# Another written-out order for the 425 pieces of layer 0, on one core

## The chip, the cores and the metric

One core of one Trainium2 chip runs the whole program in one launch. The metric is device microseconds of that core, lower is better. The engines are TensorE (PE, with its weight loads as PEld), VectorE (DVE), ScalarE (ACT), GpSimd (POOL) and SyncE (SP), which in this kernel issues nearly all DMAs. Each engine runs its own instructions strictly in the order in which the program wrote them; engines wait for each other by semaphores.

## The reference, cut to what matters

Two transformer layers with modulated layer norms, for 4 batches of 512 tokens of 512 features, in float32. The change touches the first layer alone:

```python
mod = (silu(L0_c) @ L0_wmod)            # six rows of 512 per batch: sa ca ga sb cb gb; the same for layer 1
h = layernorm(x) * (1 + ca) + sa
q, k, v = h @ Wq + bq, h @ Wk + bk, h @ Wv + bv   # 32 query heads of 16, one key and value head of 16
p = softmax(sum over heads of q (16) times k (16) per token * 1/4)   # a 16 x 16 softmax in each token
x = x + ga * repeat(p @ v, 32)
h = layernorm(x) * (1 + cb) + sb
hits = softmax(h @ centroids.T / 0.1) > 0.01      # 64 clusters
out = where(any hit of the token and any hit of the row's cluster, h @ weight.T + bias, 0)
x = x + gb * out
```

Layer 1 (grouped attention with 32 heads of 128 on 256-wide halves of the weights, then a gated feed-forward) follows, and takes over nine tenths of the time.

## The kernel before

Layer 0 is cut into 425 pieces, each a method of a class `Pieces` (L393 to L780). A string holds them in one order, and the program emits them in just that order under a manual schedule; nothing reorders them afterwards:

```python
def play(order):
    for o in order:
        name, _, eng = o.partition("/")
        name, *numbers = name.split(".")
        getattr(first_pieces, name)(*map(int, numbers), *([eng] if eng else []))
```

So the string is five queues folded into one: for each engine, the pieces that run on it, in the order in which they stand. What a piece waits for is found when it is emitted (data written by another piece, or a buffer still read by one). A piece that must wait holds up everything behind it on its engine, and nothing on the others that does not need it.

In a name such as `xn.1.2.3` the numbers are: the norm (1 before attention, 2 before the feed-forward, 3 the first norm of layer 1), the batch, and the tile or chunk of 128. In `M.0.4` they are the layer and which of the six modulation rows. The batches go in the order 0, 2, 1, 3. A suffix `/d` puts a piece on DVE.

| engine | pieces, with the line that the profile shows |
|---|---|
| SP, issue of DMAs | `x` a batch of the input, 1 MiB (L401; `x.0` is issued by ACT) · `wm.l.j` a modulation weight, 1 MiB (L406, three buffers, so each waits for the `M` that read the one three before) · `c` the two condition inputs (L396, L397) · `wq`, `wkv`, `wffn`, `cent`, `b2`, `asg` weights and small inputs · `gw` writes a gate row to DRAM (L546), `gs` reads it back spread over all partitions (L154) · `wl` first raw weights of layer 1 |
| PE | `M` modulation product (L494) · `MT` its transpose (L509) · `T` four 128 x 128 transposes of the normed x (L596) · `Q` narrow q, k, v product (L373, with h1n) · `Qt` back to tokens (L388) · `oT` (L684) · `ad` attention output spread into two tiles (L695) · `L`, `Lt` the same as `Q`, `Qt` for the clusters · `G` gate row (L538) · `F` feed-forward product of a tile, nine matmuls (L751, L755) · `hit`, `rs` |
| DVE | `st` layer-norm statistics of a tile (L62, L63) · `ve`, `nm` (L570, L579) · `silu` (L455 to L457) · `wcat`, `bcat`, `biasr` weight and bias preparation (L461, L466, L472 to L475) · `mo`, `gr` modulation and gate rows (L522, L530 to L533) · `qe`, `s`, `mx`, `den`, `rec`, `os`, `o` the small softmax (L632, L640, L649, L662, L671, L675, L678) · `xa` adds into x (L701) · `lm`, `ld`, `qs`, `fs`, `sel`, `cs` |
| ACT | `siluexp` (L451) · `xn` normed tile (L587) · `ev` a transposed chunk out of PSUM, modulated (L618; `/d` L616) · `pc`, `qc`, `lc`, `oe`, `gc`, `re` copies out of PSUM (L360) · `exp`, `le` |
| POOL | `pw` power -0.5 of the variance (L574) · `sub`, `mul` of the small softmax (L653, L666) · `R` masks a gate row (L557) · `asgf` · `fa` adds x (L765; `/d` on DVE) |
| ACT, POOL and SP | `ws` one step of the split of layer 1's weights |

Buffers that bind: PSUM has two banks for `Q`, `Qt`, `MT`, `G`, `L`, `Lt`, three for `M` (a pair of rows each), `ad` and `F`, two for `T` and `oT`. The normed tiles of norm 1 have one buffer, so `xn.1` of a batch waits for the last `T.1` of the batch before. In `modT` the rows `mo.0.0` and `mo.0.1` are what every `ev.1` needs. `R.b` needs the gate row that `gs.0.2.b` brings, and `ad.b` needs both `R.b` and `oe.b`.

After the string a short second list (four more `T`, `F`, `fs` and `fa`) leads over into layer 1, whose work is written by other code (from L1327) that the change does not touch.

## Time and profile before

| | |
|---|---|
| time, median of 3 runs | 1996.34 us (1993.04 to 2001.08) |
| the profiled execution | 1994.15 us, its span 1992.1 us |
| mean granted TensorE clock | 0.994 |
| PE busy over the span | 1943.3 us, 98% |
| DVE, ACT, POOL busy | 1185.3, 1105.1, 969.2 us |
| first PE instruction | 13.35 us |
| first matmul of layer 1 (L919) | 175.13 us |

The span is the time from the first to the last instruction of the profiled execution; some 2 us lie around it. Times inside the profile are microseconds from the start of the span. Layer 0 is the stretch up to about 175 us. A row of the timeline merges neighbouring instructions of one line: start, length, engine and line, operation, output and input, count, and in brackets the idle time before it with what ended that.

### The profile page before, as it was taken

The page shows a single profiled execution, that of the slowest core. Times are in us where ns is not written, and L with a number is a line of the kernel's source. Part 1 is how long each engine was busy: PE and PEld are TensorE (multiplying, and loading weights), DVE is VectorE, ACT ScalarE, POOL GpSimd, SP SyncE. Part 2 cuts the span into 40 slices and gives each one's busy share as a digit, 9 for nine tenths or more (in the row PEclk, how much of TensorE's full clock was granted, in tenths as well). Part 3 has the DMA queues.
Part 4 walks back from the last instruction along what each step waited for, and adds up shares of the span by engine and source line. Part 5 has one row for each costly group of instructions (what it writes and reads, how often), then busy time and mean ns, then how long its engine had stood idle before and what let it go on. Part 6 is the DMA issues. An engine that isn't in the chain of part 4 may idle for free.

```text
span 1992.1 us, 27490 instructions
## 1 busy us (share of the span) xinstructions
PE 1943.3 (98%) x8543; PEld 1466.5 (74%) x8543; DVE 1185.3 (60%) x3128; ACT 1105.1 (55%) x2541; POOL 969.2 (49%) x778
## 2 busy tenths in 40 slices
PE   5899899999999999999999999999999999999998
PEld 2345677777777777777777777777777778788887
DVE  5767655655656675565566655656555564655544
ACT  4434866666665666666666656665666652332322
POOL 2315555555557655555675555558555543711010
PEclk9799999999999999999999999999999999999999
DMA  9302667676567766656677665666656566501000
GB/s 317 113 27 74 182 166 185 161 188 167 149 161 184 188 180 170 163 153 163 179 193 197 158 164 149 151 156 179 166 142 164 136 157 216 169 26 33 25 25 23
DMA packets 268652, 293.84 MB, mean 148 GB/s; under 512 B 27218, under 2 KB 224914, under 8 KB 268500
## 3 DMA queue, kind: packets, MB, share of 16 engines
q1 hardware_dynamic: 267972, 290.97, 54.9%
q8 instruction: 71, 1.16, 0.2%
q10 hardware_dynamic: 528, 1.05, 0.1%
q14 instruction: 81, 0.66, 0.1%
HBM read 142.99 MB, written 11.57 MB: 78 GB/s over the span
## 4 chain that ended last, share of the span: by engine, by line
PE 89%; POOL 3%; DMA 3%; SPq 2%; DVE 2%; issue 1%; ACT 0%; ACTq 0%; DVEq 0%; POOLq 0%
PE quarter L862 19%; PE av L1067 14%; PE x L919 14%; PE sc L1018 13%; PE p L902 8%; PE p_up L1586 4%; PE p_gate L1586 4%; PE acc L1605 4%; PE x L902 3%; PE ffn L751 3%; SPq L1057 2%; PE narrow L373 1%; DMA x<-in_L_attn_x_dram 1%; PE lnT L596 1%; PE add_ps L695 1%
## 5 line engine op out<-in xcount | busy, mean ns | idle before, releaser
L1021 DVE CUSTOM_DVE_ANT_0 sc<-sc,mask 128x512 f32<-128x512 f32 (+3 forms) x512 | 250.0, 488 | 261.4 <-PE sc L1018 261.3
L1018 PE MATMUL sc<-kT,qT 128*128 128x512 f32 (+3 forms) x1024 | 359.2, 433 | 0.0
L1067 PE MATMUL av<-x,v 128*128 128x512 f32 x1008 | 292.2, 433 | 1.7 <-DMA x<-x 1.2
L1067 PEld LDWEIGHTS av<-x,v 128*128 128x128 f32 x1008 | 188.3, 189 | 111.1 <-issue 61.2
L1035 ACT ACTIVATE p<-p,sums 128x512 f32<-128x512 f32 (+3 forms) x256 | 143.1, 559 | 120.9 <-DVE sums L1034 120.7
L1018 PEld LDWEIGHTS sc<-kT,qT 128*128 128x128 f32 x1024 | 186.5, 190 | 30.0 <-issue 0.7
L988 DVE TENSOR_TENSOR acc<-acc,quarter 128x512 f32<-128x512 f32 x196 | 134.5, 686 | 105.9 <-PE quarter L862 105.8
L310 POOL TENSOR_TENSOR lo_qa<-raw,hi_qa 128x512 fp32r<-128x512 f32 x64 | 81.6, 1276 | 236.4 <-ACT hi_qa L309 182.1
L1035 ACT ACTIVATE x<-x,sums 128x512 f32<-128x512 f32 (+3 forms) x256 | 142.8, 558 | 83.2 <-DVE sums L1034 83.2
L862 PEld LDWEIGHTS quarter<-wo,oT 128*128 128x128 f32 x720 | 136.4, 190 | 49.1 <-issue 24.4
L862 PE MATMUL quarter<-wo,oT 128*128 128x256 f32 x720 | 170.2, 379 | 0.3 <-ACT oT L1072 0.3
L1024 ACT ACTIVATE x<-sc,sums 128x512 f32<-128x512 f32 (+3 forms) x256 | 133.4, 521 | 42.0 <-DVE sums L1021 39.3
L1038 DVE STREAM_TRANSPOSE p<-p 128x512 f32<-128x512 f32 (+3 forms) x256 | 129.1, 504 | 45.8 <-ACT p L1035 45.7
L1038 DVE STREAM_TRANSPOSE x<-x 128x512 f32<-128x512 f32 x248 | 125.6, 506 | 36.9 <-ACT x L1035 36.0
L1024 ACT ACTIVATE p<-sc,sums 128x512 f32<-128x512 f32 (+3 forms) x256 | 132.0, 516 | 14.7 <-DVE sums L1021 14.6
L310 POOL TENSOR_TENSOR lo_qb<-raw,hi_qb 128x512 fp32r<-128x512 f32 x64 | 82.0, 1283 | 115.5 <-ACT hi_qb L309 112.0
L931 DVE SCALAR_TENSOR_TENSOR qT<-p,qT 128x512 f32<-128x512 f32 x128 | 88.0, 690 | 81.1 <-PE p L902 81.1
L1072 ACT COPY oT<-av 128x512 f32<-128x512 f32 x128 | 74.5, 582 | 84.8 <-PE av L1067 84.6
L320 POOL TENSOR_TENSOR hi_qa<-hi_qa,lo_qa 128x512 fp32r<-128x512 f32 x64 | 82.5, 1290 | 75.6 <-PE x L919 75.3
L320 POOL TENSOR_TENSOR hi_qb<-hi_qb,lo_qb 128x512 fp32r<-128x512 f32 x64 | 82.9, 1296 | 66.6 <-PE x L919 64.2
L862 PE MATMUL quarter<-so,soT 128*128 128x256 f32 x480 | 113.5, 379 | 0.0
L298 ACT ACTIVATE lo_kv<-lo_kv 128x512 fp32r<-128x512 f32 x64 | 40.2, 628 | 128.4 <-POOL lo_kv L310 128.4
(265 smaller groups left out, 4295.3 us busy)
## 6 DMA issues: line engine op xcount, KB each, us to landing
x<-p SPq DMA_DIRECT2D x512, 128.0 KB, 2.6
x<-x SPq DMA_DIRECT2D x496, 128.0 KB, 2.8
raw<-in_L_attn_w_q_dram SPq DMA_DIRECT2D x128, 256.0 KB, 3.2
wo<-in_L_attn_w_o_dram SPq DMA_DIRECT2D x30, 1024.0 KB, 5.9
wm<-in_L_wmod_dram SPq DMA_DIRECT2D x12, 1024.0 KB, 9.7
raw<-in_L_attn_w_k_dram SPq DMA_DIRECT2D x32, 256.0 KB, 3.8
raw<-in_L_attn_w_v_dram SPq DMA_DIRECT2D x32, 256.0 KB, 4.0
xn<-x_d SPq DMA_DIRECT2D x28, 256.0 KB, 4.7
```

The lines of the kernel that those rows point to most:

```text
L310: nc.gpsimd.tensor_tensor(lo, w, hi.bitcast(F32), SUB)
L320: nc.gpsimd.tensor_tensor(hi, hi.bitcast(F32), lo.bitcast(F32), SUB)
L862: nc.tensor.matmul(ps[:, m, :], l[:, k, m * P : (m + 1) * P], r[:, k, :], start=(k == 0), stop=(k == 1),)
L902: nc.tensor.matmul(ps[:, m * width : (m + 1) * width], still(l, k, m), moving(r, k), start=(i == 0 and k == 0), stop=(i == len(pairs) - 1 ...
L919: nc.tensor.matmul(banks[j], l[:, k, cols], r[:, k, :], start=(half == k == 0), stop=(half == 1 and k == KC - 1),)
L1018: nc.tensor.matmul(ps[:, :w], q[:, i * P : w], kT[n][:, :w], start=True, stop=True)
L1021: nc.vector.tensor_tensor_reduce(ps[:, :w], ps[:, :w], mask[:, S - w :], -1.0, -NEG, ADD, ALU.min, nmx)
L1024: nc.scalar.activation(blocks(s, i), ps[:, :w].rearrange("p (j q) -> p j q", q=BK), AF.Exp, bias=nmx, scale=-1.0, accum_out=den,)
L1035: nc.scalar.mul(p, p, rden)
L1038: nc.vector.transpose(blocks(s, i), blocks(s, i))
L1067: nc.tensor.matmul(av.rearrange("p (a n) -> p a n", a=NG)[:, :, BK * k :], vs[n][:, k, :], pT[:, k, :, P * (s % 2) + BK * k : P * (s % 2 + ...
L1586: nc.tensor.matmul(ps[kind], w[kind][:, k, c * P : (c + 1) * P], h2[b % 2][i][:, k, :], start=(k == 0 and i == 0), stop=(k == KC - 1 and i ...
```

## The change

The string of the order is replaced. It holds the same 425 pieces with the same suffixes, each once, so that every instruction and every transfer is issued as before, by the same engine; only their order on the five queues differs, and with it which buffer each one finds free. Nothing else in the program is changed.

```diff
@@ -781,39 +781,37 @@
 
 
     order = """
-    wm.0.0 x.0 st.1.0.1 c st.1.0.3 st.1.0.2 siluexp st.1.0.0 wm.0.1 ve.1.0 pw.1.0 x.2 silu nm.1.0
-    x.1 M.0.0 st.1.2.0 xn.1.0.0 M.0.1 st.1.2.1 xn.1.0.2 st.1.2.2 wkv wm.0.2
-    st.1.2.3 xn.1.0.1 ve.1.2 pc.0.1 wq MT.0.1 mo.0.1 mo.0.0 xn.1.0.3 pw.1.2 T.1.0.0 T.1.0.1 ev.1.0.0 b2
-    bcat ev.1.0.1 wm.0.3 wm.0.4 M.0.2 st.1.1.3 T.1.0.2 st.1.1.0 ev.1.0.2 x.3 T.1.0.3
-    wcat nm.1.2 ev.1.0.3/d st.1.1.2 M.0.3 xn.1.2.0 xn.1.2.2 xn.1.2.3 xn.1.2.1 st.1.1.1 ve.1.1 pw.1.1
-    Q.0 wm.1.0 pc.0.3 T.1.2.0 T.1.2.1 qc.0 MT.0.3 mo.0.3 gr.0.2 Qt.0 qe.0 wm.1.3 ev.1.2.0 G.0.2 gc.0.2 M.0.4
-    s.0 ev.1.2.1 T.1.2.2 st.1.3.1 gw.0.2 st.1.3.0 T.1.2.3 ev.1.2.3 cent nm.1.1 mx.0 gs.0.2.0 ev.1.2.2 st.1.3.3
-    Q.2 M.1.0 wm.1.4 sub.0 st.1.3.2 xn.1.1.0 xn.1.1.1 qc.2 pc.1.0 exp.0 xn.1.1.3 xn.1.1.2 Qt.2 MT.1.0 mo.0.4 mo.1.0 qe.2
-    biasr R.0 den.0 mul.0 wm.0.5 T.1.1.0 ev.1.1.0 T.1.1.1 s.2 ve.1.3 asg gs.0.2.2 ev.1.1.1 M.1.3
-    T.1.1.2 os.0 rec.0 o.0 oT.0 oe.0 mx.2 ev.1.1.2/d pw.1.3 sub.2 T.1.1.3 ad.0.0 exp.2 M.1.4 xa.0.0 xa.0.1
-    ev.1.1.3 nm.1.3 den.2 ad.0.1 xn.1.3.0 xn.1.3.2 gs.0.2.1 Q.1 xn.1.3.1 mul.2 st.2.0.0 rec.2
-    xa.0.3 xn.1.3.3 xa.0.2 qc.1 asgf pc.1.4 R.2 T.1.3.0 ev.1.3.0 wm.1.5 Qt.1 os.2
-    st.2.0.3 o.2 st.2.0.2 st.2.0.1 qe.1 oT.2 s.1 mx.1 wm.1.2 M.0.5 wffn MT.1.4 mo.1.4 mo.1.3
-    T.1.3.1 sub.1 gs.0.2.3 oe.2 wm.1.1 ve.2.0 T.1.3.2 ev.1.3.1 M.1.5 ev.1.3.2
-    pc.1.5 exp.1 den.1 rec.1 MT.1.5 gr.0.5 G.0.5 gc.0.5 gw.0.5 pw.2.0 mul.1 T.1.3.3 ad.2.0 gr.1.5 nm.2.0
-    ev.1.3.3 xn.2.0.0 Q.3 xa.2.0 xa.2.1 xn.2.0.2 G.1.5 qc.3 xn.2.0.3 st.2.2.0 xn.2.0.1 gc.1.5 gw.1.5
-    os.1 R.1 ad.2.1 Qt.3 st.2.2.1 o.1 T.2.0.0 xa.2.2 ev.2.0.0 xa.2.3 oT.1 T.2.0.1 oe.1
-    ad.1.0 T.2.0.2 st.2.2.2 qe.3 st.2.2.3 ev.2.0.1 xa.1.1 s.3 ve.2.2 ev.2.0.2 xa.1.0 T.2.0.3
-    ad.1.1 pw.2.2 xa.1.3 nm.2.2 ev.2.0.3 gs.0.5.0 mx.3 xa.1.2 M.1.2 xn.2.2.0 M.1.1 xn.2.2.2 L.0
-    st.2.1.2 xn.2.2.3 xn.2.2.1 R.3 F.0.3 lc.0 sub.3 gs.0.5.2 st.2.1.0 T.2.2.0 st.2.1.1
-    Lt.0 pc.1.1 lm.0 exp.3 st.2.1.3 T.2.2.1 le.0 den.3 ld.0 ev.2.2.0 ev.2.2.1 ve.2.1 F.0.1
-    T.2.2.2 MT.1.1 rec.3 mul.3 os.3 pw.2.1 T.2.2.3 o.3 F.0.0 ev.2.2.2 nm.2.1 hit.0 ev.2.2.3 qs.0
-    mo.1.1 gr.1.2 oT.3 xn.2.1.0 fs.0.3 xn.2.1.3 L.2 oe.3 fs.0.1 fs.0.0 xn.2.1.1 xn.2.1.2 ad.3.0 lc.2 gs.0.5.3
-    xa.3.0 T.2.1.0 G.1.2 gc.1.2 ad.3.1 Lt.2 xa.3.3 T.2.1.1 xa.3.1 F.0.2 lm.2 xa.3.2 le.2 st.2.3.3
-    st.2.3.2 ev.2.1.1 T.2.1.2 st.2.3.1 st.2.3.0 F.2.2 ev.2.1.2 ve.2.3 pw.2.3 gw.1.2 ld.2 fa.0.1/d
-    T.2.1.3 nm.2.3 ev.2.1.0 xn.2.3.0 F.2.0 qs.2 xn.2.3.3 xn.2.3.2 xn.2.3.1 ev.2.1.3/d T.2.3.0
-    L.1 fs.0.2 T.2.3.1 fa.0.0 F.2.1 lc.1 ev.2.3.0 T.2.3.2 fs.2.2 hit.2 ev.2.3.1 fa.0.2/d
-    fa.0.3/d ev.2.3.2/d T.2.3.3 Lt.1 ev.2.3.3 L.3 fa.2.2 lm.1 F.2.3 lc.3 le.1
-    gs.0.5.1 onehot Lt.3 ld.1 wl fs.2.0 hit.1 lm.3 le.3 F.3.0 ld.3 hit.3
-    fs.2.1 fs.2.3 F.3.2 qs.3 fs.3.0 qs.1 cs fa.3.0/d fa.2.0/d rs fa.2.3/d re sel.0.2 fs.3.2
-    F.1.1 sel.0.3 F.1.0 st.3.0.3 fa.2.1 sel.0.0 sel.0.1 F.1.2 ws st.3.0.1 st.3.0.2 st.3.0.0 sel.2.1
-    sel.2.3 ve.3.0 pw.3.0 ws sel.2.0 fs.1.1 ws fa.3.2/d nm.3.0 fs.1.2 F.1.3 xn.3.0.0 fa.1.2/d
-    fs.1.0 xn.3.0.1 xn.3.0.3 xn.3.0.2 ws T.3.0.0 T.3.0.2 sel.2.2
+    x.0 wm.0.0 x.2 st.1.0.2 st.1.0.1 c siluexp silu st.1.0.3 b2 st.1.0.0 M.0.0 ve.1.0 pw.1.0 st.1.2.1
+    nm.1.0 st.1.2.2 wm.0.1 xn.1.0.0 st.1.2.0 biasr xn.1.0.2 x.1 M.0.1 st.1.2.3 pc.0.1 xn.1.0.3 ve.1.2
+    MT.0.1 st.1.1.3 xn.1.0.1 T.1.0.0 wq pw.1.2 T.1.0.2 mo.0.0 mo.0.1 ev.1.0.0 wcat wm.0.2 T.1.0.3
+    ev.1.0.3/d nm.1.2 st.1.1.2 ev.1.0.2 st.1.1.1 st.1.1.0 ve.1.1 T.1.0.1 M.0.2 wkv ev.1.0.1 xn.1.2.2 Q.0
+    xn.1.2.3 bcat xn.1.2.1 wm.0.3 qc.0 wm.0.4 x.3 M.0.3 pw.1.1 xn.1.2.0 Qt.0 nm.1.1 qe.0 T.1.2.2 pc.0.3
+    ev.1.2.2 T.1.2.3 s.0 mx.0 wm.1.0 MT.0.3 T.1.2.1 ev.1.2.3 T.1.2.0 ev.1.2.1 gr.0.2 ev.1.2.0 M.0.4
+    G.0.2 wm.1.3 xn.1.1.0 mo.0.3 gc.0.2 sub.0 st.1.3.1 Q.2 exp.0 qc.2 st.1.3.0 wm.1.4 st.1.3.2 M.1.0
+    Qt.2 den.0 rec.0 pc.1.0 xn.1.1.1 qe.2 gw.0.2 s.2 xn.1.1.3 MT.1.0 mul.0 mx.2 M.1.3 gs.0.2.0 xn.1.1.2
+    os.0 T.1.1.1 T.1.1.3 o.0 ev.1.1.1 T.1.1.2 gs.0.2.2 ev.1.1.3 ev.1.1.2/d st.1.3.3 oT.0 oe.0 sub.2
+    exp.2 mo.1.0 wm.0.5 R.0 M.1.4 ve.1.3 den.2 T.1.1.0 ev.1.1.0 ad.0.0 pw.1.3 Q.1 wm.1.2 rec.2 pc.1.4
+    xa.0.1 ad.0.1 xa.0.0 nm.1.3 mo.0.4 xn.1.3.1 wm.1.5 qc.1 M.0.5 Qt.1 mul.2 st.2.0.0 st.2.0.1 xn.1.3.3
+    M.1.5 os.2 o.2 xn.1.3.0 xn.1.3.2 xa.0.3 qe.1 oT.2 s.1 R.2 oe.2 T.1.3.1 mx.1 pc.1.5 xa.0.2 T.1.3.0
+    ev.1.3.0 ev.1.3.1 st.2.0.2 wffn st.2.0.3 sub.1 MT.1.5 wm.1.1 T.1.3.2 ve.2.0 ev.1.3.2 ad.2.0 asg
+    xa.2.1 T.1.3.3 gs.0.2.3 pw.2.0 ev.1.3.3 M.1.2 exp.1 M.1.1 xa.2.0 nm.2.0 pc.1.1 MT.1.4 gs.0.2.1
+    xn.2.0.3 ad.2.1 xn.2.0.0 mo.1.3 mo.1.4 st.2.2.1 Q.3 xn.2.0.1 R.1 xn.2.0.2 qc.3 den.1 gr.0.5 xa.2.3
+    T.2.0.2 xa.2.2 mul.1 gr.1.5 os.1 T.2.0.3 ev.2.0.2 cent st.2.2.2 G.0.5 rec.1 o.1 ev.2.0.3 T.2.0.1
+    st.2.2.0 ev.2.0.1 T.2.0.0 ev.2.0.0 Qt.3 qe.3 F.0.3 gc.0.5 st.2.2.3 ve.2.2 oT.1 s.3 pw.2.2 oe.1
+    MT.1.1 G.1.5 ad.1.1 nm.2.2 gc.1.5 mx.3 xa.1.2 xa.1.3 L.0 ad.1.0 xn.2.2.1 sub.3 xn.2.2.2 xn.2.2.0
+    st.2.1.2 xn.2.2.3 xa.1.1 xa.1.0 exp.3 den.3 st.2.1.0 T.2.2.1 st.2.1.3 T.2.2.0 mo.1.1 gw.0.5 F.0.1
+    ev.2.2.0 mul.3 T.2.2.3 ev.2.2.1 T.2.2.2 st.2.1.1 ve.2.1 lc.0 os.3 ev.2.2.3 ev.2.2.2 pw.2.1 gs.0.5.0
+    gs.0.5.2 Lt.0 rec.3 lm.0 gw.1.5 nm.2.1 le.0 xn.2.1.3 xn.2.1.2 F.0.0 o.3 R.3 ld.0 oT.3 L.2 asgf qs.0
+    xn.2.1.1 fs.0.3 xn.2.1.0 oe.3 T.2.1.0 fs.0.1 ad.3.1 xa.3.2 ev.2.1.0 T.2.1.2 T.2.1.1 xa.3.3 ev.2.1.2
+    fs.0.0 st.2.3.3 ad.3.0 lc.2 onehot xa.3.1 st.2.3.2 fa.0.1/d F.0.2 T.2.1.3 ev.2.1.1 st.2.3.1 xa.3.0
+    ev.2.1.3/d st.2.3.0 fs.0.2 Lt.2 ve.2.3 gr.1.2 pw.2.3 nm.2.3 xn.2.3.2 xn.2.3.1 F.2.0 lm.2 F.2.2
+    xn.2.3.3 xn.2.3.0 G.1.2 le.2 gc.1.2 L.1 T.2.3.0 ld.2 lc.1 T.2.3.3 hit.2 ev.2.3.0 Lt.1 gs.0.5.3 lm.1
+    T.2.3.2 ev.2.3.3 T.2.3.1 ev.2.3.1 ev.2.3.2/d gs.0.5.1 F.2.1 qs.2 fs.2.2 L.3 le.1 gw.1.2 fa.0.2/d
+    F.2.3 fs.2.0 lc.3 ld.1 fa.0.0 Lt.3 hit.0 fa.2.0/d lm.3 wl le.3 F.3.0 fs.2.1 ld.3 hit.3 qs.3 fa.2.1
+    fs.3.0 hit.1 fs.2.3 cs ws ws fa.2.3/d fa.0.3/d F.3.2 rs F.1.2 fa.2.2 fs.3.2 re qs.1 F.1.0 sel.0.3
+    sel.0.2 sel.0.1 st.3.0.3 st.3.0.1 st.3.0.2 sel.0.0 st.3.0.0 sel.2.2 ve.3.0 fs.1.2 fa.3.0/d F.1.1
+    pw.3.0 nm.3.0 F.1.3 sel.2.1 fa.1.2/d xn.3.0.2 ws fa.3.2/d xn.3.0.1 fs.1.0 sel.2.3 xn.3.0.3 xn.3.0.0
+    fs.1.1 T.3.0.2 T.3.0.0 sel.2.0 ws
     """.split()
     hits = [o for o in order if o.startswith("hit.")]
     first, last = int(hits[0][4:]), int(hits[-1][4:])
```

## The prediction

> **What bounds the kernel now.** I read the page, the busy times by stage, PE's timeline in layer 0, then DVE's and POOL's where PE stood still.

> ```profile
> PE 1943.3 (98%) x8543; PEld 1466.5 (74%) x8543; DVE 1185.3 (60%) x3128; ACT 1105.1 (55%) x2541; POOL 969.2 (49%) x778
> ```

> PE has 49 us without work in the span, so an order can win only where they lie, or where its work runs slowly. By stage (PE, PEld, DVE, ACT, POOL busy; granted clock, DMA share, GB/s):

> ```profile
> 13.00:26.00 13.00, 11.01 (x48) 5.64 (x48) 7.14 (x20) 5.75 (x8) 1.71 (x2) 1.00 1.02 359
> 26.00:46.00 20.00, 16.51 (x109) 8.46 (x109) 14.11 (x33) 13.42 (x21) 4.10 (x3) 1.00 0.85 292
> 46.00:52.00 6.00, 0.43 (x1) 0.18 (x1) 5.95 (x7) 0.00 (x0) 4.28 (x2) 0.80 1.05 344
> 52.00:63.00 11.00, 10.64 (x30) 2.79 (x30) 8.51 (x16) 4.92 (x7) 5.84 (x4) 0.50 0.57 197
> 71.00:75.00 4.00, 0.29 (x2) 0.32 (x3) 3.83 (x10) 0.00 (x0) 2.82 (x2) 0.81 0.00 0
> 75.00:81.00 6.00, 6.00 (x18) 1.86 (x16) 3.63 (x7) 2.44 (x4) 0.53 (x1) 0.56 0.01 1
> 89.00:175.00 86.00, 86.00 (x314) 39.72 (x314) 60.26 (x113) 32.99 (x53) 22.61 (x17) 1.00 0.15 51
> ```

> From 89 us to the end of layer 0 PE never rests: order can gain nothing there, only lose. Before 89 it rests 30 us (59.5 busy of 90 by windows of 10), and after the rests of 46 to 52 and 71 to 75 the clock is halved. PE's timeline shows the price:

> ```profile
> 13.35 3.64 PE L494 MATMUL modps<-wm,silu_c 128*32 128x512 f32 x16 [13.35 <-DVE silu_c L457]
> 33.66 1.07 PE L494 MATMUL modps<-wm,silu_c 128*32 128x512 f32 x8
> 51.57 0.45 PE L684 MATMUL oT_ps<-ident,o 128*128 128x128 f32 x1 [5.83 <-DVE o L678]
> 59.29 3.68 PE L373 MATMUL narrow<-h1n,wcat 128*64 128x512 f32 x8
> 74.71 0.37 PE L538 MATMUL gateps<-ident,gr 128*16 128x128 f32 x1 [4.13 <-DVE gr L533]
> 90.81 1.94 PE L373 MATMUL narrow<-hT,cent 128*64 128x512 f32 x8
> ```

> A `Q` takes 3.61 us at half clock and 1.87 at full, an `M` 1.82 and 1.0 (the first row holds two; the clock column reads 1.00 there, the durations do not). Full clock came back 12 us after work resumed (63.5), and 6 us the second time. Behind the first rest stands DVE:

> ```profile
> 42.57 0.41 DVE L472 CAST b_hi<-b 2x512 fp32r<-2x512 f32 x1
> 47.16 2.30 DVE L570 TENSOR_SCALAR ve<-bnmv 128x4 f32<-128x4 f32 x1
> 51.20 0.22 DVE L678 TENSOR_TENSOR o<-os,den 128x64 f32<-128x64 f32 x1
> ```

> Ahead of `den.0` it waits for PE (`mo.0.4`, 2.66 us) and does `biasr` (2.33); `ve.1.3` takes 2.30 instead of 0.17 while POOL runs `mul.0`; `oT.0` waits for `o.0`.

> **The change part by part.** Counts and suffixes are the same, so work is unchanged; I walk the new queues by hand, each start being the latest of its engine and its inputs, with the durations of the rows above and of the same pieces elsewhere in layer 0.

> *Start, later.* `c` moves behind `x.2` on SP. `exp_c` waited for `c` until 9.52; one more MiB at 390 GB/s (20 to 30 us) is 2.7, so 12.2; table load and exp 1.5, `silu` 0.7: first `M` at 14.5 instead of 13.35. Five statistics pieces that stood before `silu` or beside it now queue behind its wait: `nm.1.0` 17.7 (was 13.73), four `xn` and `pc.0.1` end at 21.2. `biasr` (2.33) moves here; with it `mo.0.0` ends at 23.6 (was 19.8), which every `ev.1.0` awaits. `M` and the first `T` run at half clock as before.

> *Caught up by `Q.0`.* `wq` moves ahead of `wm.0.2` and `wkv`, 1.33 MiB: 25.0 less 4.5 is 20.5, so `wcat` (2.3) is no longer DVE's wait and ends at 25.9. `ev.1.0.1` ends 27.2, `M.0.2` about 28.3, `Q.0` 30.6 with the clock rising in it (was 30.67).

> *The chain of batch 0.* `qe.0` 32.6, `s.0`, `mx.0` to 35.3 (nothing now stands between them), `sub.0` 37.3, `exp.0` 38.4, `den.0` 39.6, `mul.0` 42.0. PE meanwhile does `T.1.2`, `M.0.4`, `Q.2`, `M.1.0`, `M.1.3`, two `T.1.1`, and has done by 44.25 what it had done by 45.74. `s.2` meets `mul.0`; by the 2.30 row I let it wait to the end: 43.2, `mx.2` 44.3, `os.0`, `o.0` 45.7 (was 51.3). PE's rest is 1.5 instead of 5.8. The rows bound the unknown: no wait, 44.6.

> *`R.0` and `ad.0`.* `gw.0.2` moves behind `wm.1.4`, and SP stands at `gs.0.2.0` till it has landed. Before, it landed at 39.7 behind one MiB less: 42.4; the gate row then took 4.9: 47.3. POOL has `sub.2` to 46.3. So `R.0` ends at 47.4 to 48.4, `ad.0.0` 48.6, `Q.1` 50.5 (was 62.97). These take 1.06 and 1.87, not 2.0 and 3.61.

> *`wm.1.5` on the path.* `M.1.5` moves ahead of `oT.2`. Its load waits for `M.1.4` (47.0) and follows two gate rows, `wm.0.5` and `wm.1.2`: 54.7, at worst 56.2. PE waits from 53.6: 1.2. Then `oT.2`, `T.1.3`, `MT.1.5`, `ad.2.0` 60.1, `M.1.2`, `M.1.1` (`wm.1.1` behind `wffn`, 60.1; PE comes at 61.6), `MT.1.4`, `ad.2.1`, `Q.3` 66.4 (was 80.9). DVE stands at `mo.1.3` until 63.6; `den.1` and `gr.0.5` are behind it. `gr.0.5` meets `mul.1`, ends 68.4, and PE waits 1.0.

> *`F.0.3` early.* It moves ahead of `oT.1` and covers the wait for `o.1` (73). It starts at 70.7 instead of 92.75, with 4.5 us of PE work moved behind it (`oT.1` 0.3, two `ad.1` 2.1, `L.0` 1.9, a `G`). So 92.75 - 70.7 - 4.5 = 17.5 ahead.

> *Moved at no cost.* `bcat` (0.6) goes behind `ve.1.1`, where DVE has 2 us until `qe.0`; if that were gone, 0.6. `b2` has 7 us before `biasr` reads it; `asg` and `cent` go behind `wm.1.1`, `cent` with 15 us before `L.0`, `asg` longer; late, either would hold PE one for one. `gw.0.5` leaves at 70 and its gate rows have until `fs.0.3` at 89, `R.1` at 62.5 until `mul.1` at 66. `x.0` and `wm.0.0` change places on different queues: nothing.

> *To the end.* `F.0.3`, `F.0.1`, `F.0.0` hold three banks until `fs` (`qs.0` at 89); `ad.3.1` is then the next user, at 92.7. PE waits 0.4 there, DVE is done in time for each `T.2` and `sel` (it was busy 60.26 us of the last 86, with the same work left), and `re`, now behind two `ws` on ACT, has 4 us of cover from `F.1.2`; without it each `ws` copy costs 0.6.

> The sum from PE's side: 1.5 ahead before `o.0`; rest there 4.3 less; half clock avoided, 51.6 to 80.7: `Q.1` 1.7, `Q.3` 1.2, three `ad` 2.8, `M` 0.9, `T` 0.6, 7.2 in all; rests after 69 (4.13, 0.71, 0.76, 0.54 and 0.36) less the new ones (1.2, 0.6, 1.0): 3.7. Together 16.7, against 17.5 above: I take 17. Layer 1's first matmul comes at 158 instead of 175.13, and nothing behind it is tied to absolute time. 1994.15 - 17 = 1977.2 for the execution profiled; that lay 2.2 under the median, so 1979 against 1996.34.

> [...]

> **The rivals.**

> *The load queue gives it back.* SP now stops for `gw.0.2`, then for `M.1.4` ahead of `wm.1.5`, then for `M.0.5` ahead of `wm.1.1`; it was blocked like this before (two `wm` issues took 12.58 us from 45.21). Each us that `wm.1.5` is late beyond 53.6 is one of PE. 8 us late, PE also cools: 8 - 1.2 more rest and 5 of half clock leave 5 of 17: 1991, no change to be measured. For: the gate row's 4.9. Against: everything ahead of it is 3 MiB at most.

> *Slower: the clock stays half.* If `M`, `T`, `ad` and `Qt` do not count as work for the gate, the stretch from 28 to 71, with `Q`s far apart, runs at half clock. It has 38 us of PE work (42.4 less 4.5 of rests), 30 more at half rows; 5 of rests absorb a part: 25 lost against 17 won, 2004. It decides against the change if half clock holds for over two thirds of that stretch (17 of 25). For: after 51.6 `T`, `ad` and `M` ran 8 us without bringing it back. Against: from 26 to 46 the same mix kept it at 1.00. [...]

> [...]

> **How the numbers follow.** Forecast 0.66, load queue 0.18 (a part of it still over 10 us), half clock 0.08, warm earlier 0.08. About 0.5%, 10 us, is what a measurement of this kernel can tell from no change. Faster by more: 0.66 less 0.06 in which small waits add to 8 us, plus 0.08 and 0.02: 0.70; within: 0.22; slower: 0.08. Range: downwards 17 with 3 for the clock, 1.1 for `s.2`, 3 for rests that do not come: 1971. Upwards the unknown costs (1.5, 0.9, four more meetings of DVE and POOL at 1.3 as in the 1.50 `gr`) make 1987, and the load queue 1992; half clock is left out.

> **What would show it.** Right: first `M` near 14.5, `Q.0` ending near 30.6, a rest of under 2 us before `oT.0` at about 45.8, no half clock after 31, `F.0.3` near 71, no rest from there to the first L919 near 158, and the same length from that to the end. Wrong: a rest over 3.4 us between 30 and 70, a clock under 1.00 there, `M.1.5` waiting for its load by more than 3 us, or rests among the `F`.

## The result, and the profile after

The new order takes 1979.11 us (median, 1978.11 to 1984.06) against 1996.34: ratio 0.9914, 95% interval 0.9892 to 0.9935. The forecast was 1979. The execution that was profiled took 1984.06 us, span 1982.2; it is the longest of the five, whose other spans are 1976.2 to 1978.2. Behind the string, line numbers are two smaller than before (L919 is L917).

The page's busy times of the new kernel:

```profile
PE 1940.4 (98%) x8543; PEld 1468.1 (74%) x8543; DVE 1186.3 (60%) x3128; ACT 1104.6 (56%) x2541; POOL 965.9 (49%) x778
```

The work is the same, instruction by instruction. Busy times by stage (stretch, length, PE, PEld, DVE, ACT, POOL busy; granted clock, DMA share, GB/s), the new kernel, and then the kernel before over all of layer 0:

```profile
13.00:26.00 13.00, 7.63 (x38) 4.32 (x39) 11.21 (x28) 5.79 (x9) 2.03 (x2) 0.80 1.07 368
46.00:52.00 6.00, 4.35 (x17) 1.51 (x17) 4.94 (x9) 2.47 (x4) 4.90 (x4) 0.68 0.98 343
52.00:63.00 11.00, 11.00 (x61) 4.99 (x61) 9.00 (x16) 6.12 (x10) 3.06 (x3) 0.86 0.83 292
71.00:75.00 4.00, 2.76 (x19) 2.31 (x20) 3.93 (x9) 2.62 (x5) 0.69 (x1) 1.00 0.00 0
75.00:81.00 6.00, 6.00 (x24) 2.68 (x25) 4.93 (x13) 0.96 (x3) 1.91 (x1) 1.00 0.27 90
89.00:158.00 69.00, 68.71 (x246) 32.32 (x245) 46.88 (x96) 23.35 (x39) 17.11 (x15) 1.00 0.13 41
0.00:162.12 162.12, 137.99 (x608) 65.55 (x608) 118.26 (x243) 71.33 (x111) 47.37 (x47) 0.96 0.47 159
```

```profile
0.00:175.13 175.13, 144.58 (x609) 67.18 (x609) 119.49 (x241) 71.44 (x111) 48.22 (x47) 0.94 0.43 147
```

The last row of each is the whole account: up to layer 1's first matmul, 144.58 busy and 30.55 at rest before, 137.99 and 24.13 after. Of the 13.0 us by which layer 1 starts sooner, 6.4 are rests and 6.6 are the same matmuls running at a higher clock. PE's timeline, the new kernel (start, length, engine and line, operation, tiles, count, idle time before it and what ended it):

```profile
14.83 3.22 PE L494 MATMUL modps<-wm,silu_c 128*32 128x512 f32 x16 [14.83 <-DVE silu_c L457]
28.12 1.94 PE L373 MATMUL narrow<-h1n,wcat 128*64 128x512 f32 x8
47.65 0.30 PE L684 MATMUL oT_ps<-ident,o 128*128 128x128 f32 x1 [2.43 <-DVE o L678]
50.53 2.08 PE L695 MATMUL add_ps<-ga,oT 32*128 32x512 f32 x4
52.54 3.16 PE L373 MATMUL narrow<-h1n,wcat 128*64 128x512 f32 x8
58.70 1.06 PE L494 MATMUL modps<-wm,silu_c 128*32 128x512 f32 x8
71.89 0.27 PE L538 MATMUL gateps<-ident,gr 128*16 128x128 f32 x1 [0.89 <-DVE gr L533]
74.31 3.67 PE L751 MATMUL ffn<-wffn,hT 128*128 128x512 f32 x8
162.12 1.20 PE L917 MATMUL x<-h_hi,hi_kv 128*128 128x512 f32 x4
```

The rest before `oT.0` is 2.43 instead of 5.83, the one before `G.0.5` 0.89 instead of 4.13, and `F.0.3` starts at 74.31 instead of 92.68. But `Q.1` still ran at half clock (3.16 us; `Q.2` took 1.94 at full): after a rest of only 2.43 us. DVE's timeline has four small operations that stretch beside a POOL operation (elsewhere in this trace they take 0.19, 1.23, 0.22 and 0.19 us), and POOL's has what runs beside the first, the second and the last:

```profile
35.42 1.62 DVE L533 SCALAR_TENSOR_TENSOR gr<-sg,gr 128x16 f32<-128x16 f32 x1
41.69 2.48 DVE L640 TENSOR_TENSOR s<-qkv 128x1024 f32<-128x1024 f32 x1
46.58 0.93 DVE L678 TENSOR_TENSOR o<-os,den 128x64 f32<-128x64 f32 x1
69.69 2.05 DVE L533 SCALAR_TENSOR_TENSOR gr<-sg,gr 128x16 f32<-128x16 f32 x1
```

```profile
35.06 1.93 POOL L653 TENSOR_TENSOR s<-s,mx 128x1024 f32<-128x1024 f32 x1 [4.61 <-DVE mx L649]
40.71 2.38 POOL L666 TENSOR_TENSOR s<-s,qkv 128x1024 f32<-128x1024 f32 x1 [3.71 <-DVE den L662]
69.34 2.35 POOL L666 TENSOR_TENSOR s<-s,qkv 128x1024 f32<-128x1024 f32 x1 [2.92 <-DVE den L662]
```

### The profile page after: what moved, and what is told of

Read it like the earlier page. It is cut to its first block, busy times and chain, and to the rows that moved or that the text cites. A ratio compares the mean times of both kernels' runs of the same rounds, so it can differ in the third digit from the quotient of the medians.

```text
span 1982.2 us, 27493 instructions
## 1 busy us (share of the span) xinstructions
PE 1940.4 (98%) x8543; PEld 1468.1 (74%) x8543; DVE 1186.3 (60%) x3128; ACT 1104.6 (56%) x2541; POOL 965.9 (49%) x778
## 3 DMA queue, kind: packets, MB, share of 16 engines
q10 hardware_dynamic: 528, 1.05, 0.1%
## 4 chain that ended last, share of the span: by engine, by line
PE 92%; DVE 3%; SPq 1%; POOL 1%; issue 1%; DMA 1%; ACT 1%; DVEq 0%; POOLq 0%; ACTq 0%
PE quarter L860 19%; PE x L917 14%; PE av L1065 14%; PE sc L1016 13%; PE p L900 9%; PE p_up L1584 5%; PE p_gate L1584 4%; PE acc L1603 4%; PE x L900 3%; PE ffn L751 3%; SPq L1055 1%; PE narrow L373 1%; PE lnT L596 1%; DMA c_sb<-in_L_cT_dram 1%; PE add_ps L695 0%
## 5 line engine op out<-in xcount | busy, mean ns | idle before, releaser
L1036 DVE STREAM_TRANSPOSE p<-p 128x512 f32<-128x512 f32 (+3 forms) x256 | 129.1, 504 | 45.6 <-ACT p L1033 45.5
L1022 ACT ACTIVATE p<-sc,sums 128x512 f32<-128x512 f32 (+3 forms) x256 | 131.8, 515 | 14.6 <-DVE sums L1019 14.5
L320 POOL TENSOR_TENSOR hi_kv<-hi_kv,lo_kv 128x512 fp32r<-128x512 f32 x64 | 81.7, 1289 | 63.3 <-PE x L900 41.3
```

The lines of the kernel that those rows point to most:

```text
L320: nc.gpsimd.tensor_tensor(hi, hi.bitcast(F32), lo.bitcast(F32), SUB)
L1022: nc.scalar.activation(blocks(s, i), ps[:, :w].rearrange("p (j q) -> p j q", q=BK), AF.Exp, bias=nmx, scale=-1.0, accum_out=den,)
L1036: nc.vector.transpose(blocks(s, i), blocks(s, i))
```

## The experiments

Theory A is the prediction's ledger: each rest of PE, and the half clock behind it, is a loss of its own, and the gain is their sum. If so, taking them out of the old order one at a time must give their price. Its first rival, theory B, is that the two are one loss seen twice, or none; theories C and D came out of the runs. All ratios are to the old order.

A start time in one profile is good to about 2 us only. The kernel before and five of those below have the same order up to `G.0.2`, and in their profiles it starts at 33.46, 33.14, 33.23, 34.92, 34.99 and 35.24: the clock came back, and fell, at other moments in each. So where profiles are compared, starts are also counted from the last place that two orders share.

**The old order, first chain alone.** The six steps that stood between `exp.0` and `o.0` on DVE, and `R.0` ahead of `mul.0`, go behind.

```diff
-    ... MT.1.0 mo.0.4 mo.1.0 qe.2 biasr R.0 den.0 mul.0 wm.0.5 ... s.2 ve.1.3 ... os.0 rec.0 o.0 oT.0
+    ... MT.1.0 den.0 mul.0 R.0 wm.0.5 ... os.0 rec.0 o.0 mo.0.4 mo.1.0 qe.2 biasr s.2 ve.1.3 oT.0
```

> The order of before, with only the chain of batch 0 cleared on DVE and POOL: mo.0.4, mo.1.0, qe.2, biasr, s.2 and ve.1.3 go behind o.0, and R.0 behind mul.0. Theory A (half of the gain is the rest before oT.0 and the half clock that it brings): den.0 starts at 41.9 instead of 44.9, o.0 ends near 47.5 instead of 51.4, PE rests 1.8 instead of 5.8 us before oT.0, and the clock then holds through Q.1; 4 us of rest and up to 5 of half clock, 5 to 9 us in all: 1987 to 1991. The later rest before G.0.5 remains. Theory B (the gain comes from the order of PE and of the loads): under 2 us, since mx.2 and all of batch 2 stay where they were.

Measured: 1994.6 us, 0.9995 (0.9985 to 1.0005). PE's timeline:

```profile
47.31 0.30 PE L684 MATMUL oT_ps<-ident,o 128*128 128x128 f32 x1 [0.32 <-DVE o L678]
53.67 2.67 PE L695 MATMUL add_ps<-ga,oT 32*128 32x512 f32 x4 [3.00 <-DVE x L701]
56.27 3.68 PE L373 MATMUL narrow<-h1n,wcat 128*64 128x512 f32 x8
72.67 0.37 PE L538 MATMUL gateps<-ident,gr 128*16 128x128 f32 x1 [5.12 <-DVE gr L533]
91.71 2.84 PE L751 MATMUL ffn<-wffn,hT 128*128 128x512 f32 x6
```

The rest before `oT.0` is gone and 4.3 us won there; then the steps that were moved back hold up `xa.0`, PE waits 3.00 for it, `Q.1` runs at half clock all the same, and the wait for `gr.0.5` grows from 4.13 to 5.12. `F.0.3` is 1 us sooner (0.65 counted from `G.0.2`). With the six steps put there, theory A failed: 1.0 us (at most 3.0 by the interval) instead of 5 to 9.

**The old order, matmuls in the two rests.** Matmuls whose result nothing reads stand ahead of the two waits.

```diff
-    ... o.0 oT.0 ...            ... gr.0.5 G.0.5 ...
+    ... o.0 hot.9 oT.0 ...      ... gr.0.5 hot.6 G.0.5 ...
```

> The order of before, with nine matmuls of 128x320 whose result nothing reads put on PE ahead of oT.0, and six ahead of G.0.5, about 4.9 and 3.2 us of work inside the two rests of 5.83 and 4.13 us. Nothing else is changed, so only the clock can move. Theory A: no half clock from 50 to 80, 5.1 and 2.2 us of slow matmuls gone, 4 to 7 us faster, 1989 to 1992. Theory B (the stretch after the rest waits for DVE anyway, the clock is only a symptom): less than 2 us.

Measured: 1993.64 us, 0.9990 (0.9981 to 1.0000). PE's timeline:

```profile
59.92 1.94 PE L373 MATMUL narrow<-h1n,wcat 128*64 128x512 f32 x8
64.79 0.30 PE L684 MATMUL oT_ps<-ident,o 128*128 128x128 f32 x1 [1.13 <-DVE o L678]
77.42 0.27 PE L538 MATMUL gateps<-ident,gr 128*16 128x128 f32 x1 [0.38 <-DVE gr L533]
```

`Q.1` takes 1.94 instead of 3.68, but the faster PE then waits 1.13 for `o.2`, and the clock falls again from 65.57 to 72.40. `F.0.3` starts at 92.72, as before, but this execution was 1.78 late at `G.0.2` already: from there it comes 1.7 us sooner, which fits the 2.0 of the times. Theory A had said 4 to 7. Alone, the rest gave 1.0 us and the clock 2.0 in the old order, and both intervals reach the old order's time.

**The new order, clock kept up, and `o.0` sooner.** Four such matmuls ahead of `oT.0`; and, in another kernel, `os.0` and `o.0` ahead of `mx.2` with `R.0` ahead of `sub.2`.

```diff
-    ... ev.1.1.2/d st.1.3.3 oT.0 oe.0 ...
+    ... ev.1.1.2/d st.1.3.3 hot.4 oT.0 oe.0 ...
```

```diff
-    ... MT.1.0 mul.0 mx.2 M.1.3 ... os.0 T.1.1.1 T.1.1.3 o.0 ev.1.1.1 ... oe.0 sub.2 exp.2 mo.1.0 wm.0.5 R.0
+    ... MT.1.0 mul.0 M.1.3 ... os.0 T.1.1.1 T.1.1.3 o.0 mx.2 ev.1.1.1 ... oe.0 R.0 sub.2 exp.2 mo.1.0 wm.0.5
```

> The changed order, with four such idle matmuls ahead of oT.0, about 2.2 us inside its rest of 2.43 us. In the profiled execution this rest brought 6.8 us of half clock (48.8 to 55.6); of its five executions the spans were 1976.2 to 1982.2, the longest with the lowest clock. Theory A: the half clock is gone in every execution, spans 1976 to 1977.5, median 1978 with a spread under 2 us. Theory B: the same spread and median as the changed kernel, 1979 and 6 us.

> The changed order with os.0 and o.0 ahead of mx.2 on DVE, and R.0 ahead of sub.2 on POOL. In the profile of the changed kernel o.0 took 0.93 us because sub.2 ran beside it, and mx.2 stood in front of it. Theory A: o.0 ends near 45.5 instead of 47.5, PE's rest before oT.0 falls from 2.43 to under 0.7 us, no half clock; batch 2 is 2.5 us later, which the slack of 2.7 us of o.2 before oT.2 still covers: 1 to 5 us faster than the changed kernel, 1975 to 1978. Rival: the delay of batch 2 is on the path by way of den.2, mul.2 and R.2, and eats it: 1979 or more.

Measured: 1977.66 us, 0.9906 (0.9892 to 0.9920), and 1978.81 us, 0.9912 (0.9898 to 0.9925). In both profiles no half clock is left between 31 and 89 us. From `oT.0` to `F.0.3`, in the new kernel and then in the first of these two:

```profile
47.65:74.31 26.66, 25.41 (x143) 11.78 (x144) 21.78 (x46) 17.67 (x27) 11.48 (x8) 0.87 0.58 196
48.95:73.13 24.18, 22.93 (x144) 11.28 (x144) 22.22 (x46) 17.57 (x27) 11.51 (x8) 1.00 0.60 207
```

The half clock of the new kernel's profile cost 2.5 us there, most of the 3.2 by which its rows are longer; the waits are 1.25 us in both. Layer 1 starts at 160.95 and 160.88 instead of 162.12, only 1.2 sooner, because in these two executions the clock came back late at the start (at 30.67 and 30.51) and `G.0.2` was 1.3 behind. The four executions with the added matmuls lie within 1.7 us of each other where the new order's five spread over 6, as theory A said of them; the second kernel lies between its two forecasts. By their medians neither can be told from the new order.

**Three parts of the new order undone.** Theory C: up to 89 us, PE's start of the feed-forward hangs on a chain of small steps in DVE's queue, and the old order puts each link late. In the first kernel `pc.1.0`, `MT.1.0`, `mo.0.4` and `biasr` stand ahead of `den.0` again (`biasr` leaves the start for it); in the second `nm.2.0` stands behind `gr.1.5` again; in the third `F.0.3` stands behind `ad.1.0`.

```diff
-    ... Qt.2 den.0 rec.0 pc.1.0 ... MT.1.0 mul.0 ...
+    ... Qt.2 pc.1.0 MT.1.0 mo.0.4 biasr den.0 rec.0 ... mul.0 ...
```

> The new order with one thing of the old one put back: pc.1.0, MT.1.0, mo.0.4 and biasr stand ahead of den.0 again, so den.0 starts 5 us or so later (biasr 2.33, the wait for mo.0.4 about 2.7). Theory A (the ledger of the prediction: a rest before oT.0 and the half clock behind it are PE's own loss): the rest grows from 2.4 by about 5, half clock from about 52 to 64, time +5 to +9 us against the new order (1984 to 1988). Theory C (up to 89 us the start of the feed-forward hangs on the chain of small steps on VectorE, of which den.0 is a link): VectorE does the same work in total, so it gets back part of it: +2 to +5 (1981 to 1984), with F.0.3 later by as much. Rival (cover): PE has enough other work and the time is within 2 us.

```diff
-    ... xa.2.0 nm.2.0 pc.1.1 MT.1.4 gs.0.2.1 xn.2.0.3 ad.2.1 xn.2.0.0 ... T.2.0.2 xa.2.2 mul.1 gr.1.5 os.1 T.2.0.3
+    ... xa.2.0 pc.1.1 MT.1.4 gs.0.2.1 ad.2.1 ... xa.2.2 mul.1 gr.1.5 nm.2.0 xn.2.0.3 xn.2.0.0 xn.2.0.1 xn.2.0.2 os.1 T.2.0.2 T.2.0.3
```

> The new order with nm.2.0 put back behind gr.0.5 and gr.1.5 on VectorE, as it stood in the old order, with the xn.2.0 behind it and T.2.0.2 just ahead of T.2.0.3; nothing before 60 us changes. Theory C: nm.2.0 comes at about 73 instead of 65.4, the xn.2.0 and T.2.0 with it, G.0.5 and F.0.3 behind them: F.0.3 at 80 to 82, +5 to +8 us (1984 to 1987), no difference before 65 us. Rival (cover): PE does ad.2.1, Q.3 and G.0.5 meanwhile and the order behind takes it up, within 2 us.

```diff
-    ... Qt.3 qe.3 F.0.3 gc.0.5 ... oT.1 ... ad.1.1 ... L.0 ad.1.0 xn.2.2.1
+    ... Qt.3 qe.3 gc.0.5 ... oT.1 ... ad.1.1 ... L.0 ad.1.0 F.0.3 xn.2.2.1
```

> The new order with F.0.3 moved back behind ad.1.0 (it then stands about where the old order has it, behind oT.1, both ad.1 and L.0). If F.0.3 is cover, as the prediction says, TensorE now waits for o.1 (about 1.9 us before oT.1) and for the banks and xa before ad.1.1 and ad.1.0 (about 1.8), in a stretch thin enough for the clock to fall as well: +2 to +4 us against the new order without a fall (1981 to 1983), +5 to +8 with one. Rival (PE has all its work by then, place is indifferent): within 1 us.

Measured: 1983.89 us, 0.9931 (0.9914 to 0.9948); 1987.48 us, 0.9948 (0.9930 to 0.9966); 1986.38 us, 0.9947 (0.9932 to 0.9963). By the ratios these are 3.4, 6.8 and 6.6 us above the new order; the first alone is not clear of the two intervals. PE's timelines of the three, in that order:

```profile
50.29 0.45 PE L684 MATMUL oT_ps<-ident,o 128*128 128x128 f32 x1 [7.55 <-DVE o L678]
55.59 3.41 PE L373 MATMUL narrow<-h1n,wcat 128*64 128x512 f32 x8
```

```profile
75.84 0.47 PE L596 MATMUL lnT<-ident,xn 128*128 128x128 f32 x1 [5.25 <-ACT xn L587]
81.47 3.70 PE L751 MATMUL ffn<-wffn,hT 128*128 128x512 f32 x8
```

```profile
76.76 0.45 PE L684 MATMUL oT_ps<-ident,o 128*128 128x128 f32 x1 [1.86 <-DVE o L678]
78.87 2.08 PE L695 MATMUL add_ps<-ga,oT 32*128 32x512 f32 x4
80.88 3.21 PE L373 MATMUL narrow<-hT,cent 128*64 128x512 f32 x8
```

The first edit does two things. `G.0.2` starts at 34.62, 2.5 sooner than in the new kernel, as `mo.0.0` no longer waits for `biasr`; from `G.0.2` to layer 1 the kernel then takes 130.82 us instead of 125.03, 5.8 more, with the rest before `oT.0` grown by 5.1. So behind the edit theory A's price is about right, and the smaller time does not speak for theory C. In the second, `nm.2.0` comes at 74.07 and `F.0.3` at 81.47, 7.2 us later than in the new kernel (6.5 counted from `G.0.2`), as theory C said. In the third a rest of 1.86 is all that is added, and with it goes the clock, from 76.64 to 83.47: `ad.1.1` takes 2.08 instead of 1.13 and `L.0` 3.21 instead of 1.94. From `Qt.3`, ahead of which nothing is changed, layer 1 comes 4.8 later: 1.9 of rests and 2.9 of the same work at half clock. So in this profile `F.0.3` early is worth more than twice the wait that it covers: it is dense work in a stretch with little other work.

**The old order, the second limit lifted, alone and with the first.** `nm.2.0` goes ahead of `den.1`, and `G.0.5` behind `Q.3`; the second kernel has the first chain's edit too.

```diff
-    ... exp.1 den.1 rec.1 MT.1.5 gr.0.5 G.0.5 gc.0.5 gw.0.5 pw.2.0 mul.1 T.1.3.3 ad.2.0 gr.1.5 nm.2.0 ... Q.3 ... G.1.5
+    ... exp.1 pw.2.0 nm.2.0 den.1 rec.1 MT.1.5 gr.0.5 mul.1 T.1.3.3 ad.2.0 gr.1.5 ... Q.3 ... G.0.5 gc.0.5 gw.0.5 G.1.5
```

> The old order with nothing touched before 66 us: only pw.2.0 and nm.2.0 go ahead of den.1, and G.0.5, gc.0.5, gw.0.5 behind Q.3, as they stand in the new order. Theory C: G.0.5 (waiting for gr.0.5 behind den.1) no longer holds T.1.3.3, ad.2.0 and Q.3, the rest of 4.13 before it goes and with it the half clock of 73.86 to 80.69; Q.3 ends 5 us sooner, nm.2.0 comes 7 us sooner, F.0.3 near 88 instead of 92.7: -4 to -5 us (1991 to 1992). Theory A would say the same 4.13 rest and 3 of half clock, -7 (1989). Rival (the rest moves again, as it did twice): the wait for o.1 before oT.1 takes it back, within 1 us of the old order.

> The old order with both: the chain of batch 0 shortened (mo.0.4, mo.1.0, qe.2, biasr, s.2, ve.1.3 behind o.0, R.0 behind mul.0), which alone gave nothing, and nm.2.0 early with G.0.5 behind Q.3. Theory C (the links stand in series, so cutting one alone gives little and cutting both adds up): more than the sum of the two alone, -6 to -10 us against the old order (1986 to 1990), F.0.3 at 83 to 87. Theory A (each rest counts by itself): the sum of the two alone. Rival (another link, o.1 before oT.1, holds): no more than the second edit alone.

Measured: 1995.74 us, 0.9992 (0.9981 to 1.0004), and 1995.07 us, 0.9988 (0.9977 to 1.0000). Theory C failed as well: both links together gave 2.4 us, no more than the two alone (1.0 and 1.6), where 6 to 10 were forecast. Busy times by stage and PE's timeline of the first:

```profile
76.63:80.04 3.41, 2.16 (x9) 1.10 (x10) 3.31 (x10) 2.20 (x5) 1.32 (x2) 1.00 0.02 5
80.04:93.69 13.65, 13.12 (x50) 5.92 (x49) 10.88 (x22) 5.99 (x10) 3.47 (x3) 0.50 0.17 58
```

```profile
77.53 0.27 PE L538 MATMUL gateps<-ident,gr 128*16 128x128 f32 x1 [1.14 <-DVE gr L532]
90.06 3.64 PE L494 MATMUL modps<-wm,silu_c 128*32 128x512 f32 x16
```

The wait of 4.13 has become one of 1.14 (plus 0.34). But now the clock falls at 80.04 and stays at half to 93.69, so that a pair of `M` takes 3.64 instead of 1.92. The kernel before ran this stretch of `T`, `ad` and `Qt` at full clock: its own fall had come earlier and was over at 80.33. From `MT.1.5` (71.92, before 69.52), the last piece on PE that the edit does not reach, to layer 1 this kernel takes 106.06 us instead of 105.61: it rests 3.4 us less and is busy 3.9 us longer, so in this profile the clock took what the waits gave. (Up to `MT.1.5` it is 2.4 late through half clock alone, which here lasted from 45.91 to 66.39 and before from 49.60 to 63.26.) The kernel with both edits shows the same, half clock from 75.43 to 92.50. Theory D: the chain, the blocked PE queue and the clock lie over one another, and each hides the others.

**The old order with all three.** The last kernel, with matmuls ahead of `ad.0.1`, `G.0.5` and `T.2.0.1`.

```diff
+    ... hot.9 ad.0.1 ... hot.6 G.0.5 ... hot.2 T.2.0.1 ...
```

> The old order with all at once: the shortened chain of batch 0, nm.2.0 early with G.0.5 behind Q.3 (together they gave 2 us, and TensorE then ran at half clock from 52 to 63 and from 75 to 93), and matmuls whose result nothing reads to keep the clock up: nine of 0.29 us ahead of ad.0.1, six ahead of G.0.5, two ahead of T.2.0.1. Theory D (three limits lie on one another: the chain on VectorE, the blocked queue of TensorE, and the clock, which falls after short rests in a thin stretch; each hides the other two): now the full clock is worth what the half rows say, Q.1 1.7, ad and T and M behind 75 us some 7, so F.0.3 at 85 to 88 instead of 94.2, layer 1 at 167 to 170, 1985 to 1989. Rival (the old order of VectorE holds F.0.3 through xa, o.1 and nm.2.2 whatever the clock): full clock, but the rests grow by as much, F.0.3 at 91 or later, within 2 us of the kernel without these matmuls (1993 to 1996).

Measured: 1990.72 us, 0.9966 (0.9953 to 0.9978), the first edit of the old order that clearly gains: 6.8 us (4.4 to 9.4), where the parts gave 1.0, 2.0 and 1.6, with some 2 us of doubt in each. The clock was not kept up throughout: it fell for 3.41 us at 43.11, 63.59 and 70.42. `F.0.3` starts at 89.92, between the two forecasts. The expectation had one such matmul at 0.29 us; it takes 0.57 (each shows as two records), so the 17 took 9.9 us in rests of about 6, and some 4 us of `F.0.3`'s start are their own: an estimate, since no kernel with fewer was run. That each part is worth less than its rows is shown; that the whole is more than the sum of its parts (4.6), as theory D has it, lies within the doubt and is not.

**Better than the new order?** `c` ahead of `x.2`; then that with `o.0` sooner, as above, and `ev.1.1.0` ahead of `exp.2` (the second diff shows this last step alone).

```diff
-    x.0 wm.0.0 x.2 st.1.0.2 st.1.0.1 c siluexp ...
+    x.0 wm.0.0 c x.2 st.1.0.2 st.1.0.1 siluexp ...
```

> The new order with c, the two condition inputs, issued ahead of x.2, so that exp_c does not wait until 12.4. If the later start is caught up by Q.0 (as the prediction's second step says) the time is that of the new order, within 1 us. If it is not, up to the whole 2.7 us that c comes sooner: -1.5 (0 to -2.7), the first M at 12 to 13 instead of 14.8.

```diff
-    ... oT.0 oe.0 R.0 sub.2 exp.2 mo.1.0 wm.0.5 M.1.4 ve.1.3 den.2 T.1.1.0 ev.1.1.0 ad.0.0
+    ... oT.0 oe.0 R.0 M.1.4 T.1.1.0 ev.1.1.0 sub.2 exp.2 mo.1.0 wm.0.5 ve.1.3 den.2 ad.0.0
```

> The new order with what the runs before point to: c ahead of x.2 (layer 1 then began at 159.06 in the profile instead of 162.12), os.0 and o.0 ahead of mx.2 with R.0 ahead of sub.2 (160.88), and ev.1.1.0 ahead of exp.2 on ScalarE, since the kernel with os.0 first waited 1.86 us for it before Q.1. If the three add up: c 1.9, the rest before oT.0 2.0, no fall of the clock at 48.8 (about 1), nothing of it given back: layer 1 at 156 to 158, 1974 to 1977. If the chain on VectorE gives one of them back at den.1 or gr.0.5 (as each repair of the old order was given back): layer 1 at 159 to 161, the time that of the new order within 1.5 us.

Measured: 1978.6 us, 0.9903 (0.9885 to 0.9920), and 1980.18 us, 0.9911 (0.9887 to 0.9934). `c` early brings the first `M` to 11.81 and `oT.0` to 45.83, 1.8 sooner, and then PE meets the load that the prediction had on the path, that of `M.1.5`:

```profile
55.56 1.07 PE L494 MATMUL modps<-wm,silu_c 128*32 128x512 f32 x8 [1.85 <-DMA wm<-in_L_wmod_dram]
```

With all three `oT.0` comes at 43.46, 4.2 sooner, and then:

```profile
43.46 0.30 PE L684 MATMUL oT_ps<-ident,o 128*128 128x128 f32 x1 [0.47 <-DVE o L678]
51.29 1.12 PE L695 MATMUL add_ps<-ga,oT 32*128 32x512 f32 x2 [0.80 <-DVE x L701]
53.96 1.94 PE L388 MATMUL upright<-twice,narrow_sb 128*128 128x48 f32 x8 [0.56 <-ACT narrow_sb L360]
55.83 1.94 PE L494 MATMUL modps<-wm,silu_c 128*32 128x512 f32 x8
76.47 3.67 PE L751 MATMUL ffn<-wffn,hT 128*128 128x512 f32 x8
```

```profile
50.28:53.69 3.41, 2.33 (x11) 0.45 (x10) 3.38 (x8) 1.06 (x2) 3.25 (x2) 1.00 1.05 388
53.69:67.34 13.65, 13.38 (x57) 8.04 (x61) 8.91 (x17) 7.04 (x11) 4.00 (x3) 0.50 0.64 203
```

PE has caught up with its inputs, waits 0.46, 0.80 and 0.56 us within 5 us, and the clock falls for 13.65 us. `F.0.3` is later than in the new kernel, and layer 1 starts at 164.28: later than both forecasts had it. No version beats the new order by more than can be measured.

## Why the prediction was right, and where its steps were not

*Start.* First `M` 14.83 (14.5), `nm.1.0` 17.72 (17.7), `Q.0` ended 30.06 (30.6). Right against the kernel before; but the wait for `c` is not hidden, it still costs 1.8 us at `oT.0`. The clock came back within the first two `M`, at 17.49 in this execution, and was lost again from 20.90 to 27.73 after a rest of 1.91. No run shows the 3 us that the lower end of the range has for an earlier return of the clock. Shown is a first return 2.66 us after the first `M` in this execution, 12.36 after it before (at 25.71), and anywhere from 17.41 to 31.44 over the 14 profiles.

*Chain of batch 0.* `mx.0` ended at 34.99 (35.3), `exp.0` 38.62 (38.4), but `o.0` at 47.51 (45.7) and the rest is 2.43 (1.5). Missed were three `st.1.3` on DVE, which let `den.0` start 0.8 after `exp.0`, and two operations that stretch beside POOL: `gr.0.2` 1.62, which left PE 1.37 at rest, and `o.0` 0.93. `s.2` beside `mul.0` was priced rightly (2.48).

*`R.0`, `ad.0`, `Q.1`.* `R.0` ran from 47.39 to 48.44, as said. `ad.0.0` ended at 52.61 (48.6) and `Q.1` at 55.70 (50.5). This is the step that failed: "no half clock after 31". A clock under 1.00 there was one of the prediction's own signs of being wrong, and it came, from 48.21 to 55.04, behind a rest of 2.43. The 3.4 us of another of its signs is the author's figure, which no run shows; in the profile before, half clock stood behind rests of 5.83 and 4.13. `Q.1`, `ad.0.0`, `M` and `T` thus gave little of the 7.2 in that stretch, and 2.5 us were lost in this execution, as the kernel with four matmuls ahead of `oT.0` shows. With `c` early the rest there was 2.43 as well, and the clock held (last section).

*`wm.1.5` on the path.* `M.1.5` came at 58.70 and did not wait at all: PE was later. The step itself was right: the kernel with `c` early, in which PE is there 5 us sooner, waits 1.85 for this load until 55.56 (54.7 was said). The load-queue rival has no place in the trace. Nor has the slower one, in which `M`, `T` and `ad` keep the clock at half: the granted clock was 1.00 over the 34 us from 55.04 to 89 in which they ran.

*`gr.0.5` meets `mul.1`.* It did (2.05), and PE rests 0.89 and 0.35; 1.0 was said.

*`F.0.3` early.* 18.4 ahead, less the 4.5 of moved work, is 13.9 instead of 17.5, for the two errors above. The late-`F.0.3` kernel shows that the step was right and priced by the wrong half: the waits it covers are 1.9, the clock it holds up 2.9.

*To the end.* One rest of 0.29 us between `F.0.3` and layer 1. "The same length from there" was not quite so: 1820.1 instead of 1817.0, with the clock falling three times inside layer 1 in this execution (at 198.39, 232.53 and 1631.99) and once before (1643.63).

*The sum.* In the two profiled executions layer 1 starts 13.0 sooner, not 17, and the spans differ by 9.9; the medians differ by 17.2. So the sum was 4 us too large for these two executions, and something that the ledger lacked made it up. Among the 71 executions of the old order timed beside these runs, the span grows by some 0.9 us with each 0.001 that the mean clock falls (0.6 to 1.2 in the four rounds), between 0.993 and 0.984; its middle is 0.991, its profiled one 0.994. The new order's five lie at 0.993 to 0.999, middle 0.996, its profiled one 0.993. By that slope some 5 of the 17 go with the higher mean clock (an estimate): the profiled execution of before hid a part of this, and that of after gave a part back. That the errors cancel to 0.1 us is luck. Two slips in the working change nothing: the 0.36 among the "rests after 69" lies at 52.37, and the lower end of the range adds up to 1972.

*The ledger itself.* As an account of one profile it holds (6.4 of rests and 6.6 of clock, where it had 9.5 and 7.2). As a list of things that can be had singly it does not: chain, queue and clock removed one at a time gave 1.0, 1.6 and 2.0 us of the old order, all together 6.8. Taken out of the new order, the chain, `nm.2.0` and `F.0.3` cost 3.4, 6.8 and 6.6: 16.8 in all, close to the whole gain. This supports that the gain is theirs, but the first is not clear of noise and no kernel lacks all three, so it is no proof. An old order that reaches the new one's time by known steps was not built, and what the missing 10 us are stays open; `F.0.3`, left late there, is the first candidate.

## What to carry to other kernels

Where rests of the busiest engine lie in a row behind one serial chain, do not add their prices: remove one and look where the next wait opens before counting it. In a stretch where TensorE has short rests (0.46 to 1.86 us here), dense work that can be pulled in is worth the rest that it covers and the clock that it holds up, and the second can be the larger: for `F.0.3` they were 1.9 and 2.9 us. Compare several executions, by span and mean clock, before a single profile's difference is explained, and count starts from the last place that both orders share.

## What the runs showed of the hardware

```profile
44.80:48.21 3.41, 0.98 (x9) 0.48 (x11) 3.38 (x5) 0.60 (x3) 2.71 (x2) 1.00 0.97 348
```

```profile
40.84:44.26 3.42, 2.13 (x19) 1.27 (x12) 3.38 (x3) 1.79 (x3) 1.00 (x2) 1.00 0.28 74
44.26:47.67 3.41, 1.84 (x15) 0.74 (x15) 3.34 (x8) 1.23 (x2) 2.52 (x3) 1.00 0.91 302
```

All 55 returns, the first of each profile among them, follow a step with at least 2.66 us of work. The shortest half clock lasted one step, as from 43.09 to 46.50 in the old order with the first chain alone; from 53.69 in the kernel with all three steps of "Better than the new order?" it lasted four, with PE busy 13.38 of 13.65 us.
